# A two-layer graph network: first transpose on TensorE, earlier second loads, products one head group at a time

## The chip, the cores and the metric

The kernel runs on one core of a Trainium2 chip. The metric is the device time of one execution in microseconds (us), the median of several runs. A core has five engines that run side by side and wait for each other by semaphores: TensorE (PE in the profile; its weight loads are PEld), VectorE (DVE), ScalarE (ACT), GpSimd (POOL) and SyncE (SP), which here only issues transfers (DMA).

## The reference

The input is 64 graphs of 256 nodes with 256 features each and a 0/1 adjacency matrix per graph; all is float32. Two layers follow each other.

```python
# layer 0: twice graph attention, then a feed-forward block
def _gat(h, adj, W, a, out_features):
    Wh = jnp.matmul(h, W)
    Wh1 = jnp.matmul(Wh, a[:out_features])
    Wh2 = jnp.matmul(Wh, a[out_features:])
    e = jax.nn.leaky_relu(Wh1 + jnp.swapaxes(Wh2, 1, 2), negative_slope=0.2)
    att = jax.nn.softmax(jnp.where(adj > 0, e, NEG), axis=1)
    return jnp.matmul(att, Wh)
h = _gat(_gat(x, adj, W1, a1, F), adj, W2, a2, F)
h = _layernorm(x + h, g_ln1, b_ln1)
x = _layernorm(h + relu(h @ w_ff1 + b_ff1) @ w_ff2 + b_ff2, g_ln2, b_ln2)      # inner width 1024
# layer 1: attention with 8 heads of 32, values by relation, then a feed-forward block
scores = einsum('bhid,bhjd->bhij', q, k) / sqrt(32)
attn = softmax(scores, axis=-1)
for r in range(4):
    out = out + einsum('bhij,bhjd->bhid', attn * (adj == r), v_r)
x = _ln(src + out @ Wo + bo, g1, beta1)
x = _ln(x + gelu(x @ W1 + b1) @ W2 + b2, g2, beta2)                            # inner width 1024
```

## The kernel before

Two graphs form a pair, and each of the 32 pairs goes its whole way: first graph-attention layer, second one, feed-forward, attention, feed-forward. Up to three pairs are on their way at once. The order of the instructions on each engine is planned in Python while the program is built: a way is a generator that yields what its next piece of TensorE work waits for; `put` hands a piece of work to another engine with an estimated duration; `run` always takes the engine that can start first, and on it the piece with the lowest `rank` and then the earliest `ready`. On the chip every engine then runs its pieces in exactly that order. Only one pair at a time may be in the stage "gat", one in "attention" and one in "ff", and "ff" goes last where several pairs could use TensorE.

```python
MS = 8
START = {"tensor": 12.0, "vector": 11.0, "scalar": 12.0, "gpsimd": 0.0, "sync": 33.0}
...
    free = {name: [0.0] * n for name, n in (("bank", 8), ("a", 2 * HQ), ("m", MS), ("yb", 2), ("yT", 3), ("yTa", 1),
                                             ("xT", 1), ("adjT", 4), ("x", 5))}
...
        def x():
            to["x"] = io.tile([P, 4, D], F32, name="x", bufs=5)
            nc.sync.dma_start(to["x"], t["x"][rows].rearrange("b (c p) d -> p (b c) d", p=P))

        if at is None:
            return to, [put("sync", 0.5, emit, rank=3, lag=4.0, needs=emit.__name__) for emit in (xT, adjT, x)]
        for emit in (xT, adjT, x):
            takes(emit.__name__)
            emit()
        return to, [at_time(at)] * 3
```

`load` issues a pair's three inputs of 512 KB on SyncE: xT, adjT and x. There is one buffer for xT. With a time given (`at`) they are issued at once where the call stands, otherwise they are planned with rank 3.

A graph-attention layer needs, in every partition, the rows of exponentials of its addends. The first pair makes them with TensorE (L316), later pairs send them through memory (`store`, `spread`), which SyncE issues:

```python
        there = put("scalar", 0.6, exps, *there, rank=0, function="exp")
        if pair == 0:
            yield [there], None, 4
            rows, copied = work.tile([P, 8, 4, 32], F32, name="rows"), []
            ...                                            # L316: transposes by TensorE; L319: copies by ScalarE
            return rows, ratio, copied
        ...
        there = put("vector", 0.2, turn, there, rank=0)
        there = put("sync", 0.4, store, there, rank=0, lag=1.9)
        return rows, ratio, [put("sync", 0.4, spread, there, rank=0, lag=3.8)]

    def gat_weights(y, at, rows, ratio, there, to, empty, b):
        e = work.tile([P, 2, N], F32, name="e", bufs=2)
        ...                                                # weigh: L348, L350, L353 on VectorE; scale: L358 on ScalarE
        weighed = [put("vector", 0.9 + 0.1 * j, lambda j=j: weigh(j), *there, rank=0) for j in range(2)]
        return e, put("scalar", 0.85, scale, *weighed, rank=0)

    def gat_layers(pair, to, loads):
        yield loads[:1], "gat", 2
        ...                                                # L383: xT by w12, L374: evacuation by ScalarE
        rows, ratio, there = yield from addends(y, there, D + 2, 0, pair)
        e = [gat_weights(y, D + 2, rows, ratio, [emptied, *there], to, empty, b) for b in range(2)]
        ...                                                # L397: first layer's products
        rows, ratio, there = yield from addends(z, there, D, 1, pair)
        e = [gat_weights(z, D, rows, ratio, there, to, empty, b) for b in range(2)]
        normal = {}
        for b in range(2):
            yield [e[b][1]], None, 1
            ...                                            # L408: second layer's products
            added = add_rows(to["x"], ps, b, took(1.73), loads[2])
            transposed(to["x"], layernorm(to["x"], ln[0], b, added, biased[0]), normal, b)
        done_with("gat")
        return normal
```

`add_rows` (L419) and `layernorm` (L431 to L441, with one power on GpSimd, L444) run on VectorE. The rows are then transposed for the next matmul in three steps: 32 x 32 blocks on VectorE, a store to memory, four gathers back:

```python
    def transposed(y, ready, to, b):

        blocks = home = None

        def turn():
            nonlocal blocks
            blocks = work.tile([P, 8, 2, 32], F32, name="yb", bufs=2)
            nc.vector.transpose(blocks, y[:, of_graph(b), :].rearrange("p k (g i) -> p g k i", g=8))

        def store():
            nonlocal home
            home = scratch.tile([P, 512], F32, name="home")
            nc.sync.dma_start(home, blocks.rearrange("p g k i -> p (g k i)"))

        def gather():
            if b == 0:
                to["yT"] = work.tile([P, 2, 4, KC * 64], F32, name="yT", bufs=3)
            for q in range(4):
                nc.sync.dma_start(to["yT"][32 * q:32 * q + 32, b],
                                  home[:, 128 * q:128 * q + 128].rearrange("(a j) n -> j a n", a=4))

        there = put("vector", 0.65, turn, ready, needs="yb")
        there = put("sync", 0.4, store, there, lag=2.1, frees=["yb"])
        to[b] = put("sync", 1.75, gather, there, *([to[0]] if b else []), lag=2.1, needs=None if b else "yT")
```

`feed_forward` reads yT in L483 and makes the second product in L499. Attention works on head groups `n` (graph `n // 2`, four heads each). Scores and products use a quarter of TensorE's array at a time, scores with 32 rows (L549), products with 32 columns (L573):

```python
        def products(n):
            b, c = divmod(n, KC)
            po = bank()
            for e, out, of in ((a[n], slice(N, 2 * N), None), (a[n], slice(0, N), 0), (m[n], slice(0, N), 1)):
                for jc in range(2):
                    for o in range(HQ):
                        at = 0 if of is None else of * D + (c * HQ + o) * DH
                        nc.tensor.matmul(po[o * DH:(o + 1) * DH, out], lhsT=ones if of is None else v[b][:, jc, at:at + DH],
                                         rhs=e[o][:, jc * N:(jc + 1) * N], start=jc == 0 and of != 1, stop=jc == 1 and of != 0)
            there = took(2.63)
            frees_at(there.time, ["a"] * HQ + ["m"] * HQ)
            ...                                            # L583, L584, L580: reciprocal, product, check on VectorE
...
        scores(0)
        yield [], None, 1
        ready[1].append(projected(qT, 1, yT, wq, bqs, SCALE))
        yield [], None, 1
        ready[1].append(projected(kT, 1, yT, wk, bk, 1.0))
        yield [], None, 1
        valued.append(values(v[0], 0, 1, yT))
        yield ready[1], None, HQ
        scores(1)
        divided = []
        for n in (0, 2):
            yield [*masked[n], *masked[n + 1], *valued[:2 + n]], None, 2
            divided += [products(n), products(n + 1)]
            if n == 0:
                for jc in range(2):
                    yield [], None, 1
                    valued.append(values(v[1], 1, jc, yT))
                frees_at(clock["tensor"], ["yTa"])
                for later in (2, 3):
                    yield [], None, HQ
                    scores(later)
        frees_at(masked[3][-1].time, ["adjT"])
        for b in range(2):
            yield divided[2 * b:2 * b + 2], None, 1
            into_rows(b)
        done_with("attention")

```

`projected` is L520, `values` L512 and `into_rows` L593. The weights are loaded in the order of the code, and some additions on VectorE prepare them; they are planned for the times in `landed`:

```python
    loaded = {0: load(0, 11.0)}
    ln = [layernorm_weights("L0_gnn_g_ln1", "L0_gnn_b_ln1", "L0_gnn_b_ff2")]
    ff0 = (weights("L0_gnn_w_ff1p"), column("L0_gnn_b_ff1"), weights("L0_gnn_w_ff2"))
    ln.append(layernorm_weights("L0_gnn_g_ln2", "L0_gnn_b_ln2", "L1_gnn_bo"))
    wq, wk = weights("L1_gnn_Wqp"), weights("L1_gnn_Wkp")
    wv = const.tile([P, KC, 2, D], F32, name="wv")
    ...                                                    # attention's weights, ln[2], ff1's weights, ln[3]
    biased = [put("vector", 0.4, lambda gbm=gbm: nc.vector.tensor_tensor(gbm[1], gbm[1], gbm[2][0], ALU.add), landed[name])
              for gbm, name in zip(ln, ("ln0", "attention", "attention"))]
    differences = [put("vector", 0.4, lambda v=v: nc.vector.tensor_tensor(v[:, 1], v[:, 1], v[:, 0], ALU.subtract),
                       landed["attention"]) for v in (wv[:, 0], wv[:, 1], bv.rearrange("p (r m) -> p r m", r=2))]
...

    def whole_way(pair):
        to, loads = loaded.pop(pair)
        if pair + 1 < NPAIR:
            loaded[pair + 1] = load(pair + 1)
        normal = yield from gat_layers(pair, to, loads)
        if pair == 0:
            yield [landed["ff0"]], None, 1
            put("vector", 0.0, lambda: None, relieve(ff0[1], ff0[0], ln[0][2]), event=relieved[0])
        yield from feed_forward(to["x"], normal, ff0, AF.Relu, relieved[0], ln[1], True)
    ...
    run((whole_way(pair) for pair in range(NPAIR)), 3)
```

`relieve` is a row of narrow matmuls (L667) that takes a bias through the weights once.

Of the kernel before, what the change touches and what calls it, by code (L numbers as in the profile page):

```python
# [26 lines left out]
MS = 8  # L27
# [4 lines left out]
def two_layers(ctx: ExitStack, tc: tile.TileContext, t: dict, out: bass.AP, flag: bass.AP):  # L32
# [91 lines left out]
    def bank():  # L124
# [13 lines left out]
                                             ("xT", 1), ("adjT", 4), ("x", 5))}  # L138
# [125 lines left out]
    def load(pair, at=None):  # L264
# [17 lines left out]
        for emit in (xT, adjT, x):  # L282
            takes(emit.__name__)
            emit()
# [3 lines left out]
    def addends(y, there, at, layer, pair):  # L288
# [6 lines left out]
        ratio, rows, at_home = small.tile([P, 4], F32, name="ratio"), None, {}  # L295
# [14 lines left out]
        if pair == 0:  # L310
            yield [there], None, 4
            rows, copied = work.tile([P, 8, 4, 32], F32, name="rows"), []
# [9 lines left out]
            return rows, ratio, copied  # L322
# [9 lines left out]
        def spread():  # L332
            nc.sync.dma_start(rows.rearrange("p q n c -> p (q n c)"),
                              at_home["row"].rearrange("j q c -> (j q c)").partition_broadcast(P))

        rows = work.tile([P, 8, 4, 32], F32, name="rows")
        there = put("vector", 0.2, turn, there, rank=0)
        there = put("sync", 0.4, store, there, rank=0, lag=1.9)
        return rows, ratio, [put("sync", 0.4, spread, there, rank=0, lag=3.8)]

    def gat_weights(y, at, rows, ratio, there, to, empty, b):

        e = work.tile([P, 2, N], F32, name="e", bufs=2)
        sums, rs = small.tile([P, 2], F32, name="sums"), small.tile([P, 2], F32, name="rs")

        def weigh(j):
            k = 2 * b + j
            nc.vector.scalar_tensor_tensor(e[:, j].rearrange("p (q c) -> p q c", q=8), rows[:, :, 2 * b + 1],  # L348
# [6 lines left out]
        def scale():  # L355
            for j in range(2):
                k = 2 * b + j
                nc.scalar.activation(y[:, k, :at], y[:, k, :at], AF.Copy, scale=rs[:, j:j + 1])  # L358

        weighed = [put("vector", 0.9 + 0.1 * j, lambda j=j: weigh(j), *there, rank=0) for j in range(2)]  # L360
        return e, put("scalar", 0.85, scale, *weighed, rank=0)

    def gat_layers(pair, to, loads):
# [3 lines left out]
        z = work.tile([P, 4, D + 4], F32, name="xw", bufs=2)  # L367
# [20 lines left out]
        frees_at(clock["tensor"], ["xT"])  # L388
        rows, ratio, there = yield from addends(y, there, D + 2, 0, pair)
        e = [gat_weights(y, D + 2, rows, ratio, [emptied, *there], to, empty, b) for b in range(2)]  # L390
        there = []
        for b in range(2):
            yield [e[b][1]], None, 2
            for i in range(2):
                ps = bank()
                for j in range(2):
                    nc.tensor.matmul(ps[:, :D + 2], lhsT=e[b][0][:, j, i * P:(i + 1) * P], rhs=y[:, 2 * b + j, :D + 2],  # L397
# [748 lines left out]
```

## Time and profile before

| | us |
|---|---|
| median of 3 runs | 3246.91 (3246.41 to 3248.22) |
| span of the profiled execution | 3244.5 |
| TensorE, VectorE, ScalarE busy | 3191.3, 2028.2, 1082.6 |
| first start of L483, the first feed-forward | 62.06 |
| last matmul of the last feed-forward begins its stretch | 3221.67 |

A line of the timeline has the start and the length in us, the engine, the source line, the operation, what it writes and reads, the tile form (rows*columns of the array), the shape of the moving operand, the type and the number of instructions. In brackets stands the idle time before it and what ended that. Matmuls overlap, so the time that a stretch takes is read from its start to the start of the next one. A line of the waits has the engine, the instruction that waited, what released it, and then the total in us, the number of times and the longest.

### The profile page before, as it was taken

Reading aid. Unit: us, or ns where it says so; the run is one execution under the profiler, and the core shown is the slowest. Engines: PE = TensorE matmul, PEld = TensorE weight load, DVE = VectorE, ACT = ScalarE, POOL = GpSimd, SP = SyncE. Lnnn points to the kernel's source line nnn. Section 1 sums busy time; section 2 is a strip of 40 time slices with the busy share of each in tenths; the row PEclk is TensorE's granted clock in tenths of the full one; section 3 lists DMA queues with packets and bytes.
Section 4 is the critical chain, followed back from the end, with each engine's and each line's share of the span. In section 5 each row is a group of like instructions: output and inputs, shape, how many; then the busy total and the mean of one; then the engine's idle time right before and its main releaser. Section 6 shows DMA issues by size and latency. Waiting matters only on the chain.

```text
span 3244.5 us, 45874 instructions
## 1 busy us (share of the span) xinstructions
PE 3191.3 (98%) x17518; PEld 2041.9 (63%) x17518; DVE 2028.2 (63%) x5025; ACT 1082.6 (33%) x2012; POOL 194.2 (6%) x262
## 2 busy tenths in 40 slices
PE   6999999999999999999999999999999999999988
PEld 4666755675676667556756765675566567656645
DVE  3765665656665756656566656566665766565555
ACT  2323333333243233333332432333333334323322
POOL 0000000000000000000000000000000000000000
PEclk8999999999999999999999999999999999999999
DMA  6111311220132113112201311131122013111200
GB/s 196 59 41 58 111 49 44 81 89 27 40 104 69 46 53 107 53 40 85 85 27 43 111 62 47 63 94 53 40 85 85 27 48 114 54 59 40 65 27 28
DMA packets 217442, 211.63 MB, mean 65 GB/s; under 512 B 23040, under 2 KB 175744, under 8 KB 217216
## 3 DMA queue, kind: packets, MB, share of 16 engines
q1 hardware_dynamic: 217216, 208.62, 20.5%
q8 instruction: 141, 2.31, 0.3%
q14 instruction: 85, 0.70, 0.1%
HBM read 141.18 MB, written 67.36 MB: 64 GB/s over the span
## 4 chain that ended last, share of the span: by engine, by line
PE 95%; DVE 2%; DMA 2%; SPq 1%; issue 0%; POOL 0%; ACT 0%; POOLq 0%; DVEq 0%
PE ps L499 27%; PE ps L483 27%; PE ps L573 10%; PE ps L512 7%; PE ps L520 7%; PE ps L549 4%; PE ps L397 3%; PE ps L408 3%; PE ps L383 3%; PE ps L593 3%; DVE x L441 0%; DMA w_L_gnn_w_ff<-in_L_gnn_w_ff 0%; DMA row<-blocks 0%; DVE st L431 0%; DVE x L419 0%
## 5 line engine op out<-in xcount | busy, mean ns | idle before, releaser
L483 PE MATMUL ps<-yT,w_L_gnn_w_ff1p 128*128 128x512 f32 x1024 | 454.1, 596 | 12.3 <-DMA yT<-home 12.3
L499 PE MATMUL ps<-w_L_gnn_w_ff,ff 128*128 128x256 f32 x2048 | 462.7, 382 | 0.0
L483 PE MATMUL ps<-yT,w_L_gnn_W1p 128*128 128x512 f32 x1024 | 449.9, 596 | 11.2 <-DMA yT<-home 11.2
L499 PE MATMUL ps<-w_L_gnn_W,ff 128*128 128x256 f32 x2048 | 456.1, 380 | 0.0
L499 PEld LDWEIGHTS ps<-w_L_gnn_w_ff,ff 128*128 128x128 f32 x2048 | 387.7, 191 | 71.5 <-issue 20.6
L499 PEld LDWEIGHTS ps<-w_L_gnn_W,ff 128*128 128x128 f32 x2048 | 387.4, 190 | 63.1 <-issue 11.5
L556 ACT ACTIVATE a<-ps 128x512 f32<-128x512 f32 x512 | 263.3, 606 | 469.7 <-PE ps L549 469.7
L560 DVE TENSOR_TENSOR m<-a,adjT 128x512 f32<-128x512 f32 x512 | 318.7, 686 | 116.1 <-ACT a L556 116.0
L444 POOL TENSOR_TENSOR rstd<-rstd,mhalf 128x2 f32<-128x2 f32 x256 | 193.5, 756 | 3043.9 <-DVE rstd L433 3016.3
L483 PEld LDWEIGHTS ps<-yT,w_L_gnn_W1p 128*128 128x128 f32 x1024 | 194.3, 191 | 242.9 <-issue 231.9
L514 DVE TENSOR_TENSOR v<-ps,b_L_gnn_bv 128x512 f32<-128x512 f32 x128 | 88.4, 690 | 407.9 <-PE ps L512 405.1
L483 PEld LDWEIGHTS ps<-yT,w_L_gnn_w_ff1p 128*128 128x128 f32 x1024 | 193.2, 190 | 237.0 <-issue 219.9
L486 ACT ACTIVATE ff<-ps,c_L_gnn_b 128x512 f32<-128x512 f32 x256 | 175.0, 685 | 396.0 <-PE ps L483 395.5
L419 DVE TENSOR_TENSOR x<-ps,x 128x512 f32<-128x512 f32 x256 | 175.4, 685 | 199.6 <-PE ps L499 195.2
L583 DVE RECIPROCAL s<-ps 128x256 f32<-128x256 f32 x128 | 224.4, 1753 | 121.1 <-PE ps L573 121.1
L486 ACT ACTIVATE ff<-ps,c_L_gnn_b_ff 128x512 f32<-128x512 f32 x256 | 175.7, 690 | 363.9 <-PE ps L483 363.8
L358 ACT ACTIVATE xw<-xw,rs 128x258 f32<-128x258 f32 (+1 forms) x256 | 116.4, 502 | 393.6 <-DVE rs L353 393.4
L512 PE MATMUL ps<-wv,yTa 128*128 128x512 f32 x512 | 238.7, 599 | 0.0
L431 DVE BATCH_NORM_STATS2 st<-x 128x6 f32<-128x256 f32 x512 | 208.5, 407 | 3.3
L348 DVE SCALAR_TENSOR_TENSOR e<-rows,ratio 128x256 f32<-128x256 f32 x256 | 122.1, 477 | 137.2 <-DMA rows<-row 118.2
L374 ACT ACTIVATE xw<-ps 128x260 f32<-128x260 f32 (+1 forms) x256 | 96.2, 385 | 324.0 <-PE ps L383 293.1
L512 PEld LDWEIGHTS ps<-wv,yTa 128*128 128x128 f32 x512 | 94.6, 190 | 120.3 <-issue 120.3
(95 smaller groups left out, 3435.5 us busy)
## 6 DMA issues: line engine op xcount, KB each, us to landing
home<-yb SPq DMA_DIRECT2D x192, 256.0 KB, 2.1
yT<-home SPq DMA_DIRECT2D x768, 64.0 KB, 2.0
rows<-row SPq DMA_DIRECT2D x62, 512.0 KB, 4.1
xT<-in_xT SPq DMA_DIRECT2D x32, 512.0 KB, 4.6
adjT<-in_adjT SPq DMA_DIRECT2D x32, 512.0 KB, 5.8
x<-in_x SPq DMA_DIRECT2D x32, 512.0 KB, 6.6
out<-x SPq DMA_DIRECT2D x32, 512.0 KB, 3.2
w_L_gnn_w_ff1p<-in_L_gnn_w_ff1p SPq DMA_DIRECT2D x1, 1024.0 KB, 7.8
```

The costliest lines, as they stand in the source:

```text
L419: return put("vector", 0.6, lambda: nc.vector.tensor_tensor(rows, p, rows, ALU.add), *events, frees=["bank"])
L431: nc.vector.bn_stats(st[:, j, :], rows[j])
L444: power = put("gpsimd", 0.8, lambda: nc.gpsimd.tensor_tensor(rstd, rstd, mhalf[:, :2], ALU.pow), there)
L483: nc.tensor.matmul(p1, lhsT=w1[:, c, m * P:(m + 1) * P], rhs=yT[c], start=c == 0, stop=c == KC - 1)
L486: there = put("scalar", 0.6, lambda m=m, p1=p1: nc.scalar.activation(f[m], p1, func, bias=b1[:, m:m + 1]), took(1.72), relieved, function= ...
L499: nc.tensor.matmul(p2[:, j * D:(j + 1) * D], lhsT=f[m][:, (2 * j + b) * P:(2 * j + b + 1) * P], rhs=w2[:, m, :], start=m == 0, stop=m == N ...
L512: nc.tensor.matmul(ps, lhsT=yT[:, b, c, jc * P:(jc + 1) * P], rhs=wv[:, c].rearrange("p r m -> p (r m)"), start=c == 0, stop=c == KC - 1)
L520: nc.tensor.matmul(ps, lhsT=w[:, d, c * P:(c + 1) * P], rhs=yT[:, :, d, :], start=d == 0, stop=d == KC - 1)
L556: nc.scalar.activation(a[n][o], ps[o], AF.Exp)
L560: nc.vector.tensor_tensor(m[n][o], a[n][o], adj, ALU.mult)
L573: nc.tensor.matmul(po[o * DH:(o + 1) * DH, out], lhsT=ones if of is None else v[b][:, jc, at:at + DH], rhs=e[o][:, jc * N:(jc + 1) * N], s ...
L583: there = put("vector", 1.68, lambda: nc.vector.reciprocal(s, po[:, N:]), there, rank=0)
```

## The change

The change has six parts.

- The first pair's rows after its graph attention are transposed by TensorE and copied by ScalarE (`transposed_on_tensor`), in place of the way through memory.
- The second pair's inputs are loaded right after the first feed-forward's weights, ahead of the weights of attention and of the second feed-forward.
- A pair leaves the stage "gat" after its first layer, so that the next pair's first layer can begin while the second one is under way. For this `e` has four buffers where it had two, and the plan counts buffers of `e` and `rows`.
- The two halves of the weighing of one graph are chained, where both were free to start.
- Attention's products are made for one head group at a time as its masks are ready, where both groups of a graph were made in one stretch; the second graph's scores are spread between them, and the first graph's rows are finished ahead of the last products.
- `m`, the masked weights, has seven buffers where it had eight.

The diff, cut to its core:

```diff
-MS = 8
+MS = 7
@@ load
         for emit in (xT, adjT, x):
-            takes(emit.__name__)
+            takes(emit.__name__, free[emit.__name__] != [])
             emit()
@@ addends
         def spread():
+            at_home["rows"] = rows = work.tile([P, 8, 4, 32], F32, name="rows")
...
-        return rows, ratio, [put("sync", 0.4, spread, there, rank=0, lag=3.8)]
+        return at_home, ratio, [put("sync", 0.4, spread, there, rank=0, lag=3.8, needs="rows")]
@@ gat_weights
-        e = work.tile([P, 2, N], F32, name="e", bufs=2)
...
+                of["e"] = work.tile([P, 2, N], F32, name="e", bufs=4)
...
-        weighed = [put("vector", 0.9 + 0.1 * j, lambda j=j: weigh(j), *there, rank=0) for j in range(2)]
-        return e, put("scalar", 0.85, scale, *weighed, rank=0)
+        there = put("vector", 0.9, lambda: weigh(0), *there, rank=0, needs="e")
+        there = put("vector", 1.0, lambda: weigh(1), there, rank=0, frees=["rows"] * b)
+        return of, put("scalar", 0.85, scale, there, rank=0)
@@ gat_layers
-            yield [e[b][1]], None, 2
+            yield [e[b][1], *([] if b or not pair else [through_gat[pair - 1]])], None, 2
...
+            frees_at(clock["tensor"], ["e"])
+        done_with("gat")
...
-            added = add_rows(to["x"], ps, b, took(1.73), loads[2])
-            transposed(to["x"], layernorm(to["x"], ln[0], b, added, biased[0]), normal, b)
-        done_with("gat")
+            there = took(1.73)
+            frees_at(there.time, ["e"])
+            added = add_rows(to["x"], ps, b, there, loads[2])
+            normed = layernorm(to["x"], ln[0], b, added, biased[0])
+            if pair:
+                transposed(to["x"], normed, normal, b)
+            else:
+                normal[b] = normed
+        happens(through_gat[pair], clock["tensor"])
+        if pair == 0:
+            yield from transposed_on_tensor(to["x"], normal)
@@ new
+    def transposed_on_tensor(y, to):
+        to["yT"] = work.tile([P, 2, 4, KC * 64], F32, name="yT", bufs=3)
+        takes("yT")
+        for b in range(2):
+            yield [to[b]], None, 1
+            p = bank()
+            for c in range(KC):
+                for j in range(2):
+                    for q in range(4):
+                        at = q * 64 + c * 32
+                        nc.tensor.matmul(p[32 * q:32 * q + 32, c * N + j * P:c * N + (j + 1) * P],
+                                         lhsT=y[:, 2 * b + j, at:at + 32], rhs=ident, start=True, stop=True)
+            def copy(b=b, p=p):
+                nc.scalar.activation(to["yT"][:, b].rearrange("p a (ck i) -> p ck a i", i=32),
+                                     p.rearrange("p (ck a i) -> p ck a i", a=4, i=32), AF.Copy)
+            to[b] = put("scalar", 0.55, copy, took(0.6), frees=["bank"])
@@ products, attention
-            there = took(2.63)
+            there = took(2.8)
...
-        for n in (0, 2):
-            yield [*masked[n], *masked[n + 1], *valued[:2 + n]], None, 2
-            divided += [products(n), products(n + 1)]
-            if n == 0:
-                for jc in range(2):
-                    yield [], None, 1
-                    valued.append(values(v[1], 1, jc, yT))
-                frees_at(clock["tensor"], ["yTa"])
-                for later in (2, 3):
-                    yield [], None, HQ
-                    scores(later)
+        for n in range(4):
+            yield [*masked[n], *valued[:2 + n // 2 * 2]], None, 1
+            divided.append(products(n))
+            if n < 2:
+                yield [], None, 1
+                valued.append(values(v[1], 1, n, yT))
+                frees_at(clock["tensor"], ["yTa"] * n)
+                yield [], None, HQ
+                scores(n + 2)
+            if n == 2:
+                yield divided[:2], None, 1
+                into_rows(0)
         frees_at(masked[3][-1].time, ["adjT"])
-        for b in range(2):
-            yield divided[2 * b:2 * b + 2], None, 1
-            into_rows(b)
+        yield divided, None, 1
+        into_rows(1)
@@ loads
     ff0 = (weights("L0_gnn_w_ff1p"), column("L0_gnn_b_ff1"), weights("L0_gnn_w_ff2"))
+    loaded[1] = load(1, 27.0)
     ln.append(layernorm_weights("L0_gnn_g_ln2", "L0_gnn_b_ln2", "L1_gnn_bo"))
@@ whole_way
-        if pair + 1 < NPAIR:
+        if pair + 1 < NPAIR and pair + 1 not in loaded:
             loaded[pair + 1] = load(pair + 1)
```

## The prediction

> **What bounds the kernel now.** I read the shares of the engines and the slices of the page first, then TensorE's waits, its timeline at both ends, the DMA queue's timeline, and last the lengths of single stretches in TensorE's timeline.
>
> ```profile
> PE 3191.3 (98%) x17518; PEld 2041.9 (63%) x17518; DVE 2028.2 (63%) x5025; ACT 1082.6 (33%) x2012; POOL 194.2 (6%) x262
> ...
> PEclk8999999999999999999999999999999999999999
> ...
> PE ps L483 <- DMA yT<-home: 23.4, 3, 12.3
> PE ps L397 <- ACT xw L358: 5.5, 2, 4.0
> PE ps L408 <- ACT xw L358: 2.8, 1, 2.8
> ```
>
> TensorE is busy for 3191.3 of 3244.5 us. All of its idle time is 53 us, and nearly all of that lies at the two ends: the table by stretch has it busy 2958.27 of the 2960 us from 168 to 3128. So no wait between can be worth anything; the middle changes only if TensorE's own work changes. The ends hold two sorts of loss: idle time, and half clock (the trace's clock record stands at 0.5 from 21.5 to 25.0, 31.8 to 35.2, 42.0 to 48.9, 52.3 to 65.9 and 3137.9 to 3148.2).
>
> ```profile
> 21.62 5.38 PE L397 MATMUL ps<-xw,e 128*128 128x258 f32 x16 [4.03 <-ACT xw L358]
> 31.71 5.41 PE L408 MATMUL ps<-xw,e 128*128 128x256 f32 x16 [2.81 <-ACT xw L358]
> 43.29 6.50 PE L383 MATMUL ps<-w,xT 128*128 128x260 f32 x16 [2.71 <-DMA xT<-in_xT]
> 62.06 3.75 PE L483 MATMUL ps<-yT,w_L_gnn_w_ff1p 128*128 128x512 f32 x4 [12.26 <-DMA yT<-home]
> ...
> 43.12 1.86 SPq L278 DMA_DIRECT2D x<-in_x  x1
> 49.83 0.37 SPq L270 DMA_DIRECT2D xT<-in_xT  x1
> 50.24 0.47 SPq L459 DMA_DIRECT2D home<-yb  x1
> ```
>
> The reader is to see why L483 waits 12.26 us. The first pair's transpose was cut into blocks on VectorE at 42.30, but its store was issued only at 50.24: ahead of it in the one queue stood the third pair's xT, which waits until L383 has read the second pair's xT, which itself landed at 43.3 behind all weights.
>
> Full-speed work done by 65.9 us, when the clock comes back: L116 3.8, L383 twice 3.5, L316 2.1, L397 3.5, L408 3.5, L667 3.6, four of L483 1.7, together 25. So 41 us are lost there, of which 7.5 is the very first load.
>
> ```profile
> 3106.56 3.70 PE L512 MATMUL ps<-wv,yTa 128*128 128x512 f32 x8
> 3110.19 1.15 PE L549 MATMUL ps<-qT,kT 32*128 32x256 f32 x16
> 3111.26 1.99 PE L499 MATMUL ps<-w_L_gnn_w_ff,ff 128*128 128x256 f32 x8
> 3113.19 1.15 PE L549 MATMUL ps<-qT,kT 32*128 32x256 f32 x16
> ...
> 3176.51 2.01 PE L549 MATMUL ps<-qT,kT 32*128 32x256 f32 x32
> 3178.45 5.42 PE L483 MATMUL ps<-yT,w_L_gnn_W1p 128*128 128x512 f32 x12
> ...
> 3183.79 1.07 PE L573 MATMUL ps<-a,ones 128*32 128x256 f32 x16
> 3189.11 1.99 PE L593 MATMUL ps<-w_L_gnn_Wo,oT 128*128 128x256 f32 x8
> 3190.94 1.89 PE L499 MATMUL ps<-w_L_gnn_W,ff 128*128 128x256 f32 x8
> 3192.67 1.89 PE L593 MATMUL ps<-w_L_gnn_Wo,oT 128*128 128x256 f32 x8
> ```
>
> These give the price of a change of tile form, read from start to next start. Eight of L499 among their like take 1.73; between two L549 stretches they take 3113.19 - 3111.26 = 1.93, so entering and leaving cost 0.20. L549 takes 1.07 for 16 and 1.94 for 32: 0.87 for each further 16, hence 0.2 of its own per stretch. L573's stretch of 96 takes 5.32 (3183.79 to 3189.11), and its inner groups of 16 follow each other at 0.865, so 5.32 - 6 x 0.865 = 0.13 of its own. **A stretch of L573 more therefore costs 0.13 + 0.20 = 0.33 us, a stretch of L549 more 0.4 us.**
>
> **What the skill says.** "TensorEngine Tiling (Array Packing)", Key Properties: changing the tiling mode, not only the tile, drains TensorE. The trace agrees and puts 0.33 to 0.4 us on going in and out. "TensorE: Matmul & The Clock Gate", What's actually happening: TensorE runs at half clock after an idle window of about 3.4 us and is released after one of work. The trace agrees: its clock record changes in steps of 3.41 us, and L397 takes 5.38 at the start against 3.48 later. "DMA: Bandwidth & Descriptors", Anatomy of one DMA: a semaphore wait happens on the issuing sequencer before dispatch. The trace agrees: SyncE stands from 44.98 to 49.83 at xT, and everything after it waits too.
>
> **The change, part by part.**
>
> 1. *First transpose by TensorE.* Removes two stores and eight gathers (issued from 50.24, landed 61.8). Adds 32 matmuls of 128 columns in 128x32 form: L573's 256 columns come at 0.054 each, so 0.027 each, 0.9 us in all with the form change 1.2; and two ScalarE copies at 0.6 like L533's. After the last layernorm (43.8) L483 needs about 1.2 + 0.6 us. In itself this moves L483 from 62 to about 46, less what L667's bias products (3.6 us, put after the transposes) push it back: 49.
>
> 2. *Second pair's loads before attention's weights.* xT, adjT and x (1.5 MB) follow the first feed-forward weights, which landed at 24.05; at the 300 to 330 GB/s of the busy stretches they need 5 us, and xT is there at about 26. With the release of "gat" after the first layer, L383 of pair two (3.5 us) fills the hole before L408 and keeps the clock up: 2.7 of wait and some 4 of half clock saved. But all that follows lands 5 us later. VectorE's additions to the shifts and value weights (L655, L657) stand before the first pair's layernorm in its queue, and one waited 1.15 us for beta, till 34.63. Their planned times (31.0) are not changed, so they stay there and now wait until about 39.5: the layernorm starts near 41 instead of 35.98.
>
> 3. *Order on VectorE in the plan.* I followed the plan's own constants by hand, for order only. Pair two's weighing (rank 0) becomes due in the plan just ahead of the last steps of pair one's layernorm. In fact its rows are stored behind five loads of pairs three and four (1.9 us each between issues before, so 9.5 us after 39.3), thus spread and landed only around 56. If that order stands, pair one's layernorm is done near 61 and nearly all of part 1 is given back. I give this 60%.
>
> Sum for the start: 41 lost now; 26 to 32 if the layernorm is only held by beta, 39 to 40 if also by the rows. Weighted, a gain of 6 us; at best 15.
>
> 4. *Products one group at a time.* No arithmetic changes. Two stretches of L573 per pair become four: 2 x 0.33 = 0.66. L549 has now 106 stretches in the 29 pairs from 200 to 3000, 3.7 per pair, and will have four: 0.3 x 0.4 = 0.13. Where a score stretch comes directly ahead of a product stretch one change is shared, perhaps one per pair, 0.2 back. 0.6 us x 32 pairs = 19 us, all on TensorE, which sets the time.
>
> 5. *The end.* 9.94 us of idle at 3133.9, 1.22 at 3206.6, 2.2 of half clock. Finer products let attention finish with less feed-forward between, which leaves more of it to cover the layernorm and transpose (15.3 us from 3128.5 to 3143.8), and graph one's layernorm no longer stands in graph two's way. I take 4 us of gain; the last 9 us after 3235.7 stay.
>
> 6. *e twice as deep, m seven for eight.* Only the order of a middle without idle: 0, perhaps a few us of waits where a mask now waits for a product.
>
> **Sum:** -6 + 19 - 4 = +9 on 3246.9 is 3256. I take it down to 3253, since the finer interleaving may save more form changes than one per pair.
>
> **Rivals.** (a) *The start wins:* L483 near 46 to 49, the clock up, the end shortened by 8: -15 - 8 + 15 = 3239. For it: 12.26 is the largest wait of the run and its cause is removed. Against: one queue's wait is exchanged for another's. (b) *New waits in the middle:* seven m buffers, and VectorE needed 2.5 (masks) + 2.6 (reciprocal, product, check) + 0.7 (values) = 5.8 us per head group, against TensorE's 2.7 + 1.8 + 1.1 = 5.6 in one step of attention. If feed-forward doesn't fill, 0.5 us per pair makes 3268. Against: it fills now, without a gap. (c) *The change of form is hidden:* if stretches cost nothing more, 3237.
>
> **Range and chances.** 3238 to 3266 holds it 8 times in 10. Over 2% is 65 us: more than all idle time, and 2 us per pair of new loss the other way. Faster 0.01, same 0.97, slower 0.02.
>
> **What would show it.** L483's first start: 45 to 50 (part 1 unhindered) or near 60 (part 3). L655's wait for beta until 39 to 40. Four stretches of 48 of L573 per pair, each 2.73, with L499 around them at 0.1 more per side; a pair's period longer by 0.6 between 200 and 3000. Idle before L483 at the end under 9.94. The prediction is wrong if the period is unchanged, or if TensorE idles over 10 us between 168 and 3100.

## The result and the profile after

The changed kernel takes 3256.77 us (median of 6 runs, 3255.88 to 3258.0) against 3246.66 us (6 runs) for the kernel before, run beside it: 1.003 times as long, 95% interval 1.0017 to 1.0043. The change costs 10 us. Its profiled execution spans 3255.4 us, 10.9 more than the one before.

In what follows "lost" is the length of a stretch less the work done in it: the matmuls that the trace counts there, at the pace they have at full speed (13.733 us for 32 of 512 columns, 13.813 us for 64 of 256, a quarter of that on quarter tiles, 3.63 us for 32 of one column). What is lost is idle time, half clock (TensorE's clock record stands at 0.5) and changes of tile form. A pair's period is the distance of two pairs' output transfers, averaged over 27. For the middle it is the surer measure: at a window's edges the loss of one pair, 2.2 to 2.7 us, can fall in or out.

| | before | after |
|---|---|---|
| lost from 0 to 180 us | 46.6 | 52.6 |
| lost from 180 to 2950 us | 65.2 | 74.5 |
| lost from 2950 us to the end | 29.6 | 23.3 |
| work added by the transposes | | 1.7 |
| period of a pair | 98.83 | 99.15 |

So the start is 7.7 us worse (6.0 lost and 1.7 of work), the middle 9.3 worse, the end 6.3 better: together 10.7.

The page's engine and clock rows and TensorE's waits after:

```profile
PE 3205.0 (98%) x17582; PEld 2037.2 (63%) x17582; DVE 2018.5 (62%) x5023; ACT 1137.5 (35%) x2052; POOL 193.1 (6%) x262
...
PEclk7999999999999999999999999999999999999999
...
PE ps L404 <- ACT xw L363: 18.5, 2, 13.5
PE ps L500 <- DVE x L458: 6.2, 1, 6.2
PE ps L520 <- DMA yT<-home: 3.9, 1, 3.9
```

The wait of 12.26 us for the first transposed rows is gone, and one of 13.5 us stands in its place. The first slice is granted less clock than before (7 tenths, not 8). The lines are numbered anew. On TensorE L404 was L397, L417 was L408, L388 was L383, L500 is the transpose, L705 was L667, L520 was L483, L536 was L499, L549 was L512, L557 was L520, L586 was L549, L610 was L573, L630 was L593. On VectorE L353 and L358, parts of the weighing, were L348 and L353, and of the layernorm L436 was L419, L454 was L437, L458 was L441; L693 was L655. On ScalarE L363 was L358.

TensorE's timeline at the start of the changed kernel:

```profile
22.44 6.52 PE L404 MATMUL ps<-xw,e 128*128 128x258 f32 x16 [4.94 <-ACT xw L363]
35.39 3.72 PE L417 MATMUL ps<-xw,e 128*128 128x256 f32 x16 [2.04 <-ACT xw L363]
45.35 1.93 PE L500 MATMUL ps<-ident,x 128*32 128x128 f32 x32 [6.25 <-DVE x L458]
60.81 3.81 PE L404 MATMUL ps<-xw,e 128*128 128x258 f32 x8 [13.53 <-ACT xw L363]
64.55 1.58 PE L500 MATMUL ps<-ident,x 128*32 128x128 f32 x32
66.06 4.30 PE L705 MATMUL ps<-c_L_gnn_b_ff2c,w_L_gnn_w_ff1p 128*128 128x1 f32 x32
78.34 10.46 PE L520 MATMUL ps<-yT,w_L_gnn_w_ff1p 128*128 128x512 f32 x24
```

The first graph is transposed at 45.35, the second only at 64.55, and the feed-forward begins at 78.34 (62.06 before). Between the two, in TensorE's order, stands the second pair's L404, which waits 13.53 us. Why the second transpose could not come sooner in any case is seen in VectorE's timeline:

```profile
38.66 0.43 DVE L693 TENSOR_TENSOR b_L_gnn_beta<-b_L_gnn_beta,ff 128x256 f32<-128x256 f32 x1 [2.62 <-DMA b_L_gnn_beta<-in_L_gnn_beta]
...
44.73 0.87 DVE L458 SCALAR_TENSOR_TENSOR x<-x,rstd,b_L_gnn_b_ln 128x256 f32<-128x256 f32 x2
57.15 0.49 DVE L353 SCALAR_TENSOR_TENSOR e<-rows,ratio 128x256 f32<-128x256 f32 x1 [11.54 <-DMA rows<-row]
...
61.24 0.86 DVE L454 SCALAR_TENSOR_TENSOR x<-x,mv,b_L_gnn_g_ln 128x256 f32<-128x256 f32 x2
62.02 0.88 DVE L458 SCALAR_TENSOR_TENSOR x<-x,rstd,b_L_gnn_b_ln 128x256 f32<-128x256 f32 x2
```

L353 is the second pair's weighing. In VectorE's order it stands ahead of the last two steps of the first pair's layernorm (L454, L458) and waits 11.54 us for rows, which landed at 57. They were issued by SyncE behind pairs three and four:

```profile
39.08 0.43 SPq L270 DMA_DIRECT2D xT<-in_xT  x1
39.55 0.47 SPq L274 DMA_DIRECT2D adjT<-in_adjT  x1
40.07 2.03 SPq L278 DMA_DIRECT2D x<-in_x  x1
42.24 1.86 SPq L274 DMA_DIRECT2D adjT<-in_adjT  x1
44.15 1.37 SPq L278 DMA_DIRECT2D x<-in_x  x1
45.62 1.93 SPq L332 DMA_DIRECT2D row<-blocks  x1
53.40 0.35 SPq L336 DMA_DIRECT2D rows<-row  x1
```

The blocks were ready at 36.0; the store was issued at 45.62 and its successor waited for its landing until 53.40. In the middle TensorE's timeline shows how the products now lie:

```profile
1505.20 1.15 PE L586 MATMUL ps<-qT,kT 32*128 32x256 f32 x16
1506.28 1.07 PE L610 MATMUL ps<-a,ones 128*32 128x256 f32 x16
1507.17 1.05 PE L610 MATMUL ps<-a,v 128*32 128x256 f32 x16
1508.03 1.05 PE L610 MATMUL ps<-m,v 128*32 128x256 f32 x16
1509.01 1.98 PE L549 MATMUL ps<-wv,yTa 128*128 128x512 f32 x4
1510.92 1.15 PE L586 MATMUL ps<-qT,kT 32*128 32x256 f32 x16
```

A stretch of 48 products takes 1509.01 - 1506.28 = 2.73 us, and it follows the scores directly: this happens twice per pair. L549 between two such groups takes 1.91 us for four matmuls of 512 columns, which take 1.72 where no quarter tiles are near. At the end:

```profile
3216.34 15.56 PE L520 MATMUL ps<-yT,w_L_gnn_W1p 128*128 128x512 f32 x32 [3.86 <-DMA yT<-home]
```

Of the two waits of the end, 9.94 and 1.22 us, one of 3.86 is left.

### The profile page after: what moved, and what is told of

Same layout as the page of the kernel before. It is cut to its first block, busy times and chain, and to the rows that moved or that the text cites. A ratio compares the mean times of both kernels' runs of the same rounds, so it can differ in the third digit from the quotient of the medians.

```text
span 3255.4 us, 46023 instructions
## 1 busy us (share of the span) xinstructions
PE 3205.0 (98%) x17582; PEld 2037.2 (63%) x17582; DVE 2018.5 (62%) x5023; ACT 1137.5 (35%) x2052; POOL 193.1 (6%) x262
## 4 chain that ended last, share of the span: by engine, by line
PE 97%; DMA 2%; DVE 1%; SPq 0%; issue 0%; ACT 0%; POOL 0%; POOLq 0%; DVEq 0%; ACTq 0%
PE ps L536 27%; PE ps L520 27%; PE ps L610 11%; PE ps L549 7%; PE ps L557 7%; PE ps L586 4%; PE ps L630 4%; PE ps L404 3%; PE ps L388 3%; PE ps L417 3%; DMA x<-in_x 0%; DMA home<-yb 0%; PE ps L705 0%; DMA row<-blocks 0%; DVE x L436 0%; DVE st L448 0%
## 5 line engine op out<-in xcount | busy, mean ns | idle before, releaser
L520 PE MATMUL ps<-yT,w_L_gnn_W1p 128*128 128x512 f32 x1024 | 459.4, 597 | 3.9 <-DMA yT<-home 3.9
L536 PE MATMUL ps<-w_L_gnn_W,ff 128*128 128x256 f32 x2048 | 455.5, 381 | 0.0
L536 PE MATMUL ps<-w_L_gnn_w_ff,ff 128*128 128x256 f32 x2048 | 454.1, 380 | 0.0
L520 PE MATMUL ps<-yT,w_L_gnn_w_ff1p 128*128 128x512 f32 x1024 | 445.4, 592 | 0.0
L536 PEld LDWEIGHTS ps<-w_L_gnn_w_ff,ff 128*128 128x128 f32 x2048 | 390.2, 191 | 67.1 <-issue 10.3
L536 PEld LDWEIGHTS ps<-w_L_gnn_W,ff 128*128 128x128 f32 x2048 | 386.6, 190 | 64.5 <-issue 13.2
L597 DVE TENSOR_TENSOR m<-a,adjT 128x512 f32<-128x512 f32 x512 | 328.0, 687 | 147.5 <-PE ps L610 75.6
L593 ACT ACTIVATE a<-ps 128x512 f32<-128x512 f32 x512 | 264.3, 603 | 326.9 <-PE ps L586 326.9
L520 PEld LDWEIGHTS ps<-yT,w_L_gnn_w_ff1p 128*128 128x128 f32 x1024 | 194.4, 190 | 230.8 <-issue 221.5
L520 PEld LDWEIGHTS ps<-yT,w_L_gnn_W1p 128*128 128x128 f32 x1024 | 192.6, 191 | 219.5 <-issue 209.7
L436 DVE TENSOR_TENSOR x<-ps,x 128x512 f32<-128x512 f32 x256 | 173.6, 678 | 249.0 <-PE ps L536 169.8
L353 DVE SCALAR_TENSOR_TENSOR e<-rows,ratio 128x256 f32<-128x256 f32 x256 | 122.1, 477 | 218.7 <-DMA rows<-row 182.8
L549 PE MATMUL ps<-wv,yTa 128*128 128x512 f32 x512 | 247.3, 605 | 0.0
L363 ACT ACTIVATE xw<-xw,rs 128x258 f32<-128x258 f32 (+1 forms) x256 | 114.8, 501 | 333.8 <-DVE rs L358 333.5
L549 PEld LDWEIGHTS ps<-wv,yTa 128*128 128x128 f32 x512 | 92.0, 189 | 118.2 <-issue 118.2
```

What stands on the lines that cost most here:

```text
L436: return put("vector", 0.6, lambda: nc.vector.tensor_tensor(rows, p, rows, ALU.add), *events, frees=["bank"])
L520: nc.tensor.matmul(p1, lhsT=w1[:, c, m * P:(m + 1) * P], rhs=yT[c], start=c == 0, stop=c == KC - 1)
L536: nc.tensor.matmul(p2[:, j * D:(j + 1) * D], lhsT=f[m][:, (2 * j + b) * P:(2 * j + b + 1) * P], rhs=w2[:, m, :], start=m == 0, stop=m == N ...
L549: nc.tensor.matmul(ps, lhsT=yT[:, b, c, jc * P:(jc + 1) * P], rhs=wv[:, c].rearrange("p r m -> p (r m)"), start=c == 0, stop=c == KC - 1)
L593: nc.scalar.activation(a[n][o], ps[o], AF.Exp)
L597: nc.vector.tensor_tensor(m[n][o], a[n][o], adj, ALU.mult)
```

## The experiments

Each was run in 5 rounds or more beside the kernel before, whose median was 3245.55 to 3246.65 us. "Lost" is from the one profiled execution; such an execution differs from the median of its kernel by up to 4.2 us (before_singly, where it was the slowest of 21), so small differences are judged by the medians. The 1.7 us of the transposes' work are part of every run but before_singly, and are not in "lost".

| run | us | ratio to before (95%) | lost at start, middle, end | period |
|---|---|---|---|---|
| rows_late_in_plan | 3259.55 | 1.0041 (1.0028 to 1.0055) | 53.9, 73.2, 23.4 | 99.15 |
| before_tensor_first | 3250.20 | 1.0009 (1.0001 to 1.0018) | 45.7, 68.4, 29.3 | 98.92 |
| loads_wait | 3249.05 | 1.0008 (1.0 to 1.0017) | 45.7, 74.3, 23.8 | 99.15 |
| loads_wait_rows_late | 3246.41 | 1.0002 (0.9993 to 1.001) | 39.7, 73.9, 24.9 | 99.15 |
| weights_late_after | 3245.22 | 0.9998 (0.9989 to 1.0006) | 41.0, 73.6, 23.3 | 99.14 |
| after_in_stretches | 3261.30 | 1.0044 (1.0031 to 1.0058) | 50.7, 76.2, 28.3 | 99.25 |
| before_singly | 3250.89 | 1.0012 (1.0006 to 1.0019) | 47.9, 77.5, 24.8 | 99.31 |
| before_new_start | 3244.94 | 0.9996 (0.9988 to 1.0004) | 42.7, 67.5, 27.6 | 98.86 |
| new_start_all_singly | 3249.39 | 1.0013 (1.0004 to 1.0021) | 45.7, 76.2, 23.3 | 99.27 |
| new_start_last_singly | 3237.54 | 0.9975 (0.9967 to 0.9983) | 38.9, 68.2, 22.5 | 98.86 |
| weights_late_in_plan | 3230.63 | 0.9957 (0.9943 to 0.9971) | 32.0, 67.7, 22.0 | 98.82 |

### The start: is it VectorE's order, the rows, or a lack of work?

**rows_late_in_plan.** The planned order alone, in the changed kernel:

```diff
-        ... put("sync", 0.4, spread, there, rank=0, lag=3.8, needs="rows")]
+        ... put("sync", 0.4, spread, there, rank=0, lag=18.0 if pair == 1 and layer == 0 else 3.8, needs="rows")]
```

> The changed kernel, but the plan is told that the second pair's first rows land 14 us later than it thinks (a lag of 18 us for 3.8), which is about what the trace shows. Only the order of the queues changes. Theory (VectorE's order costs the start): the first pair's layernorm comes ahead of the second pair's weighing and ends near 47 in place of 62.9, L520 begins near 52 in place of 78.3, TensorE's wait of 13.5 us before L404 is gone, and the time falls by 10 to 14 us to about 3244. Rival (the late rows or the later loads themselves bind the start, whatever the order): the idle time moves to another instruction before 100 us and the time stays within 3 us of 3257.

On VectorE the layernorm came first, as meant (its last L458 begins at 45.19), and the time did not fall. TensorE's timeline:

```profile
44.23 3.25 PE L500 MATMUL ps<-ident,x 128*32 128x128 f32 x64 [5.45 <-DVE x L458]
51.61 16.74 PE L520 MATMUL ps<-yT,w_L_gnn_w_ff1p 128*128 128x512 f32 x32
69.91 3.65 PE L404 MATMUL ps<-xw,e 128*128 128x258 f32 x16
113.17 6.39 PE L417 MATMUL ps<-xw,e 128*128 128x256 f32 x16 [13.59 <-ACT xw L363]
```

L520 begins at 51.61, 26.7 us sooner, and the wait of 13.5 us before L404 is gone; but one of 13.59 us has come up at L417, 52 us later. When the first pair's feed-forward ends, at 92.4, little else is ready: bias products and the third pair's L404, until 99.6. The first pair's rows are on their way through memory to attention (122.8), the second pair, whose L404 came only at 69.91, has its feed-forward at 119.4, and next in TensorE's order is the third pair's L417, which waits for its own rows. The rival was right: the wait moved. The first start of L520 was a poor measure of the start.

The run is not VectorE's order alone, though. The plan's later time for the rows also put the second pair's scaling on ScalarE, and its L404 on TensorE, behind the first pair's L520:

```profile
59.32 0.17 DVE L358 RECIPROCAL rs<-sums 128x2 f32<-128x2 f32 x1
67.25 1.70 ACT L363 ACTIVATE xw<-xw,rs 128x258 f32<-128x258 f32 x4
```

The weighing was done at 59.5 and the scaling began at 67.25. So some 8 us of the second pair's lateness are the new order's own, and what VectorE's order alone is worth with late rows is not shown.

**before_tensor_first.** The transpose alone (`transposed_on_tensor` as in the change), in the kernel before:

```diff
-            transposed(to["x"], layernorm(to["x"], ln[0], b, added, biased[0]), normal, b)
+            normed = layernorm(to["x"], ln[0], b, added, biased[0])
+            if pair:
+                transposed(to["x"], normed, normal, b)
+            else:
+                normal[b] = normed
         done_with("gat")
+        if pair == 0:
+            yield from transposed_on_tensor(to["x"], normal)
```

> The kernel before with nothing but the first pair's transpose by TensorE; the loads stay where they were. Theory: the wait of 12.26 us is gone, L483 begins near 52 (after L383 of the second pair, which still waits for xT until 43.3), total about 3236. Rival (the wait is only handed on: the second pair's rows, which still land near 60, or SyncE's blocked queue hold TensorE next): idle time of near 10 us turns up at L397 or later, total within 3 us of 3247.

L509, this kernel's L483, begins at 54.77 and 12.26 us of wait are gone, yet the run is 3.5 us slower than before. Half of the rival holds: 5.27 us of idle time come up at the third pair's L397 at 104.34, and half clock after it; the start loses 45.7 where it lost 46.6, with 1.7 of work added. Of the 3.2 that the middle loses more, 2.3 are four waits at L397 of at most 0.7; the rest isn't explained.

**loads_wait** and **loads_wait_rows_late.** The rows sooner, in the changed kernel; then VectorE's order as well (a lag of 10.0):

```diff
-        return to, [put("sync", 0.5, emit, rank=3, ...
+        return to, [put("sync", 0.5, emit, *([at_time(40.0)] if pair in (2, 3) else []), rank=3, ...
```

> The changed kernel, but the loads of pairs three and four are planned no sooner than 40 us, so that SyncE issues the store and the spread of the second pair's rows ahead of them. Theory (the start is bound by the second pair's rows, which land at 57 behind those loads): the rows land near 47, L404 of the second pair begins near 49 in place of 60.8, all that follows comes 10 us sooner, total 3245 to 3249. Rival (TensorE lacks work in the first 120 us because of the depth of each pair's chain, whatever the rows do): a new wait of about 10 us at L404, L417 or L520 before 120 us, total over 3253.

> The same, and the plan is told of a lag of 10 us for these rows (3.8 before), which puts the first pair's layernorm ahead of the second pair's weighing on VectorE. Theory (both orders matter, and the late rows came first): L520 begins near 52, L404 of the second pair lies inside it, no wait over 4 us between 50 and 120 us, total 3242 to 3247. Rival (the layernorm's place is the cause, and the run with it alone failed for another reason): this run is over 5 us faster than the one with the loads alone.

The first of them is a clean test: SyncE alone has another order than in the changed kernel, the four other engines have the same instructions in the same order to the end. The second pair's weighing finds its rows at 48.98 (57.15 in the changed kernel), its L404 begins at 52.65 (49 was expected) after a wait of 6.42 us, the time falls to 3249.05, 7.7 us below the changed kernel, and the only wait that follows in the first 125 us is 0.44 us. With both, the start loses 39.7 and the time is 3246.41, as expected. The new order, which brought nothing alone, brings 2.6 us now (the medians of 13 runs each; the intervals overlap, and the loss at the start, 45.7 to 39.7, points the same way). So the rows' lateness was the cause of most, and the order, of VectorE and with it of ScalarE and TensorE, its second part.

**weights_late_after.** The third suspect, the additions that wait for beta, moved behind the layernorm by planning attention's weights later, on top of the run before:

```diff
-    landed = ... ("attention", 31.0), ...
+    landed = ... ("attention", 41.0), ...
```

> The changed kernel with the loads of pairs three and four behind the second pair's rows, the rows' lag told to the plan, and attention's weights planned for 41 us. Theory: the addition L436 near 37.5 in place of 40, L520 near 49 in place of 51.7, 1 to 3 us off 3246.4. Rival: within 1 us of it, since the second pair's rows set the pace from there on.

L436 begins at 37.69 (40.08 in the changed kernel), as expected, but L520, expected near 49, only at 54.96 (51.71 in the run before), and the time is 1.2 us lower, which the intervals don't tell from nothing. In its profiled execution L705 shows where such a gain can go:

```profile
42.98 1.17 PE L500 MATMUL ps<-ident,x 128*32 128x128 f32 x32 [3.61 <-DVE x L458]
48.11 6.99 PE L705 MATMUL ps<-c_L_gnn_b_ff2c,w_L_gnn_w_ff1p 128*128 128x1 f32 x32
54.96 8.45 PE L520 MATMUL ps<-yT,w_L_gnn_w_ff1p 128*128 128x512 f32 x12
```

Half clock lasted from 44.0 to 61.1 there, and the 32 narrow matmuls took 6.99 us, against 3.88 in the run before (loads_wait_rows_late).

### The middle: what does a split stretch cost?

**before_singly.** The kernel before with the changed kernel's loop over `n` and nothing else:

> The kernel before with nothing but the products one head group at a time (eight m buffers kept). Theory: start as before (L483 at 62.1), time per pair longer by 0.33 us (10 us in all), end shorter by about 6 us, total about 3251. Rival (the end is shorter because the next pair's first layer begins sooner, not because of the products): the end stays as it was, with near 10 us of idle at 3134, and the total is 3257. Second rival (form changes cost nothing): 3241 to 3247.

The middle loses 77.5 where it lost 65.2, the period is 99.31 where it was 98.83, the end loses 24.8 where it lost 29.6, and the time is 3250.89. Both signs and the sum came as expected. The cost per pair, 0.47, is more than the 0.33 that I took from the whole change; but it is read from that kernel's slowest execution, and the medians differ by only 4.2 us where the parts make 8.8, so it may be too high. The end is shorter here without the earlier release of the stage, so the first rival is out.

**after_in_stretches.** The changed kernel with the old loop, eight m buffers, and e three deep in place of four, to fit the memory:

> The changed kernel with the products of both head groups of a graph in one stretch again (eight m buffers; e has three in place of four, to fit). Theory (changes of tile form set the cost of the middle): TensorE's time per pair between 200 and 3000 us falls by 0.33 us from 99.15 back to 98.8, 10 us in all; part of the gain at the end (6 us) is lost again, so 3248 to 3253. Rival (the middle is longer because the layers of two pairs overlap, or because of the m buffers): the time per pair stays at 99.1 and the total at 3257.

This missed: 3261.30, with a middle of 76.2; the rival, a period that stays near 99.1, came closer (99.25). Worked out from the trace, two things went against the saving; no run tests them. A pair has no fewer changes of form: with the old loop the four score stretches stand alone beside two product stretches, six groups, and the changed kernel also has six (the kernel before has 5.7), since two of its four product stretches follow scores directly. Only the stretches' own 0.14 us is saved, twice per pair, some 8 us. And new short waits came up: TensorE idles for 4.7 of the 2770 us (1.3 in the changed kernel), and its 56 stretches of 32 of L520 take 13.829 us on average, not 13.733. So in a kernel that leaves the stage early and has three buffers for `e` the old loop is no cheaper than the new one. The end lost its gain (28.3). As e is one shallower, the run doesn't tell the earlier release from the depth of e, nor what the deeper e is worth.

**before_new_start, new_start_last_singly, new_start_all_singly.** The kernel before with the transpose by TensorE, the second pair's loads early and pairs three and four from 52 us on; then with the products split in the last two pairs; then in all (and planned with 2.8 us each, as in the change, in place of 2.63):

```diff
+    loaded[1] = load(1, 27.0)                      # after ff0's weights, as in the changed kernel
-        ... put("sync", 0.5, emit, rank=3, ...
+        ... put("sync", 0.5, emit, *([at_time(52.0)] if pair in (2, 3) else []), rank=3, ...
@@ in the other two; new_start_all_singly takes the second branch always
+        if pair < NPAIR - 2:
             for n in (0, 2):          # the old loop: both head groups of a graph
             ...
+        else:
+            for n in range(4):        # the changed kernel's loop
+            ...
```

> The kernel before (products in stretches, stage left after the second layer) with three things of the start: the transpose by TensorE, the second pair's loads ahead of attention's weights, and the loads of pairs three and four planned no sooner than 52 us. Theory: first L483's counterpart near 50, the loss of the first 180 us falls from 47 to about 33, the middle and the end stay, total 3233 to 3237. Rival (the wait is handed on again, as with the transpose alone): total over 3242.

> The kernel of the run before this one, with the products one head group at a time in the last two pairs only. Theory (products one at a time shorten the end and cost 0.33 us per pair): 4 to 6 us less than that run, with no wait of near 10 us at 3125 to 3145, total 3228 to 3233. Rival (the end depends on the order of all pairs before it, and the gain of the end doesn't come with the last two alone): no difference within 2 us.

> The kernel before with the new start and the products one head group at a time in all pairs: all of the change but the earlier release of the stage and the deeper e. Theory (each split product stretch costs TensorE 0.2 to 0.33 us; the release adds nothing in the middle): against the same kernel with only the last two pairs split, 10 to 13 us more between 180 and 2950 us, total 3246 to 3250. Rival (the middle's cost in the change comes from the release and the buffers): within 3 us of 3237.5.

The first one is only as fast as the kernel before (3244.94): its start loses 42.7, not 33. A wait of 3.82 us came up at the third pair's L397 (103.14) and the clock fell to half there, and the half clock before it lasted from 43.0 to 60.1. The rival was right again, in part. Splitting the last two pairs brings 7.4 us, more than expected: the end falls from 27.6 to 22.5, and 3.8 us lie in the start, where every engine of both kernels has the same order of instructions (idle time differs by 1.4 us; half clock before 180 us lasts 30.8 and 17.0 us). The total, 3237.54, is above the 3228 to 3233 expected, since the kernel under it was. Splitting all pairs then costs 11.9 us, as expected: the period rises from 98.86 to 99.27, 11 us over 27 pairs (8.0 in the middle's window), with no earlier release of the stage in it. So in kernels without that release the middle's cost is the split stretches', shown twice (98.83 to 99.31 and 98.86 to 99.27).

**weights_late_in_plan.** The fastest of these with attention's weights planned for 41 us, by the same edit as in weights_late_after:

> The fastest kernel so far (new start, last two pairs split), with attention's weights planned for 41 us in place of 31, so that the additions L655 and L657 stand behind the first pair's layernorm on VectorE. Theory (the layernorm was held by beta for 2.98 us there): the layernorm's first addition near 36 in place of 38.81, L509 near 48, 1 to 3 us off 3237.5. Rival (TensorE's waits only move, as they did with the transpose alone): within 1 us of 3237.5.

```profile
33.36 0.69 DVE L425 TENSOR_TENSOR x<-ps,x 128x512 f32<-128x512 f32 x1 [1.33 <-PE ps L408]
...
49.29 8.54 PE L509 MATMUL ps<-yT,w_L_gnn_w_ff1p 128*128 128x512 f32 x16
92.48 3.67 PE L509 MATMUL ps<-yT,w_L_gnn_w_ff1p 128*128 128x512 f32 x8
95.99 3.64 PE L397 MATMUL ps<-xw,e 128*128 128x258 f32 x16
```

3230.63 us, the best of all: 0.9957 of the kernel before, and below the changed kernel by 26 us. That is 6.9 us less than the same kernel without this edit, where 1 to 3 were expected. The layernorm's first addition (L425, this kernel's L419) starts at 33.36 (38.81 there), yet L509 only 1.5 us sooner, so the expected part is small. The larger part was not foreseen: the plan now puts eight of the second pair's L509 at 92.48, ahead of the third pair's L397, where the run without the edit waited 3.79 us and lost clock; the start loses 32.0 where it lost 38.9.

## Why the prediction was right

The range, 3238 to 3266, holds 3256.77, and the signs of the middle and the end were right. That the sum (+9, taken down to 3253 for the forecast) is so near the measured +10 is luck: the start came out 14 us worse than its term, the middle 10 us better and the end 2 us better.

*Part 1, the transpose.* Mis-sized by a factor of two: 0.9 us of work were put down, and it is 1.7. L573's pace of 0.054 is per counted matmul, and the trace counts two for each product, so the 32 products are 64 matmuls; they took 3.25 us together where they came partly at half clock. "In itself this moves L483 to 49" was nearly borne out where the loads came early too (51.61 in rows_late_in_plan); the transpose alone brought 54.77, behind a wait of 4.39 us for the second pair's xT.

*Part 2, the loads.* Right in mechanism, too large in size: beta was awaited until 38.66, not 39.5, and the layernorm began at 40.08, not 41. L388 did fill the hole before L417, and L417 then took 3.72 us, not 5.41.

*Part 3, the order.* Right: the weighing stood ahead of L454, the rows landed at 57 (56 was said), the layernorm was done at 62.9 (61 was said). But **the sum for the start was mis-sized: a gain of 6 was put down, and it was a loss of 7.7.** Two things were wrong in it. I took 60% for what then came in full, and counted 39 to 40 of loss for it, where 45.0 were lost by 65.9 us and another 3.6 by 110 (42.9 and 42.7 in the kernel before, by the same count): the clock stood at half through the new wait (41.7 to 65.6) and again behind L705 (69.0 to 75.9). And I took for granted that without the order's harm 10 to 15 us would be won. rows_late_in_plan shows 13.59 us of new wait instead: the gain needs the second pair ready as well. With its rows sooner the start loses 39.7 (loads_wait_rows_late), and in weights_late_in_plan 32.0, where the kernel before lost 46.6.

*Part 4, the products.* Right in mechanism, mis-sized in the term for shared changes: I credited one shared change per pair, and there are two. 0.66 + 0.13 - 0.4 = 0.39 us per pair, where 0.6 was predicted; measured are, by the periods, 0.32 in the whole change, 0.47 and 0.40 for the products alone. Taken as the loss of a pair over the same 27 periods, without idle time, they are 0.37, 0.44 and 0.41, so the whole change is hardly cheaper than the products alone. In total 9 to 10 us in place of 19. The "0.33 to 0.4 us on going in and out" is the price of a whole stretch: going in and out is 0.20 of it (1.93 us for eight L499 at 3111.26 us in the kernel before, 1.73 without it), and the rest is the stretch's own.

*Part 5, the end.* 6.3 us where 4 was put down. before_singly gives 4.8 of them without the earlier release, and new_start_last_singly 5.1 with two pairs split, so most of it is the products' finer order.

*Part 6.* Right in size: 1.3 us of idle time in the middle, with seven m buffers. No run changes the buffers, the earlier release or the chained weighing alone.

*The rivals.* (a) failed because one queue's wait was exchanged for another's, as its counter-argument said. (b), new waits in the middle, didn't come. (c), changes of form that cost nothing, is refuted by the period.

## What to carry to other kernels

When TensorE is busy without a gap, as here, the waits at the start are worth removing only if the next pair's work is ready too: remove one, then look where the next idle time stands before believing the gain. In a plan with fixed order, times that the plan has wrong (a landing 14 us later than it thinks) do harm on engines that have nothing to do with the transfer. Splitting a stretch of quarter-array matmuls is a cost per stretch. Pay it where nothing else covers the wait for the result (in the last two pairs: the end lost 22.5 us, not 27.6), not in the steady middle (11.9 us lost).

## What the runs showed of the hardware

The same 32 one-column matmuls (L667 before, L705 after) took 3.63 us in the kernel before and 3.88 to 6.99 us in the other twelve executions, by where the half clock fell.

They may also bring it about. A second stretch of 32 of them comes in the steady flow, beginning at 153 to 172 us; in the kernel before it is this one:

```profile
164.70 3.63 PE L667 MATMUL ps<-c_L_gnn_b2c,w_L_gnn_W1p 128*128 128x1 f32 x32
```

TensorE was not idle in the 20 us before it in any of the 13 executions, and yet in 12 of them the clock record falls to 0.5 between 2.3 and 4.7 us after the stretch begins, for 3.4 or 6.8 us (168.3 to 171.7 in the kernel before). From 181 to 2950 us no execution has any half clock. So here half clock came without idle time, while the prediction speaks of it only after idle time. That the one-column matmuls are the cause is inferred; no run leaves them out.

Two kernels with the same order of instructions on every engine up to 3095 us lost 42.7 and 38.9 us in the first 180 us. So a few us of a start are the clock's, and a gain of 1 to 3 us there can't be read from one profile.
